# Selective scan with channels and states on partitions, inputs spread by DMA

## The chip, the cores and the metric

One core of a Trainium2 chip. The metric is the device time of one execution in microseconds (us), as the median of several. Kernels are compared only within the same rounds. On one core, a run is called slow when it lies over 1.5% above the fastest of its kernel.

## The reference

Eight images of 256 channels and 32 x 32 pixels go through four layers, each behind a group norm and with a residual: attention of 8 heads, two 3x3 convolutions, and a mixer. The mixer has, per image, four Mamba branches of 64 channels (128 inside), then gates, pointwise products and another attention. The part that matters here, once per branch and image (32 times):

```python
dA  = jnp.exp(dt[..., None] * A)                 # 128 channels x 16 states
dBu = (dt * u)[..., None] * Bm[:, :, None, :]
def step(h, inp):                                # over 1024 pixels
    dA_t, dBu_t, C_t = inp
    h = dA_t * h + dBu_t
    return (h, jnp.einsum('bds,bs->bd', h, C_t))
```

## The kernel before

One state at a time, 128 channels on the partitions, all in float32. Per state: B comes by DMA as one row copied to 128 partitions; ScalarE makes the decays; TensorE makes C on all partitions in PSUM; GpSimd forms dt*u*B; VectorE scans and multiplies by C; TensorE adds the states up through an identity.

```python
def spread(s):
    hs, da, c_all = work("hs"), work("da"), big_tile()
    nc.sync.dma_start(out=hs[:, 0:N], in_=b_rows[s : s + 1].to_broadcast([P, N]))
    nc.scalar.activation(da[:, 0:N], dd, AF.Exp, scale=a_neg[:, ...])      # cut
    for h in range(2):
        nc.tensor.matmul(c_all[:, HALVES[h]], mxpw[...].to_broadcast([P, P]),
                         u[:, HALVES[h]], start=True, stop=True)           # cut
    nc.gpsimd.tensor_mul(hs[:, 0:N], du[:, 0:N], hs[:, 0:N])
    return hs, da, c_all
# for each of 16 states:
nc.vector.tensor_tensor_scan(hh, da[:, 0:N], hh, 0.0, ALU.mult, ALU.add)
nc.vector.tensor_mul(hh, hh, c_all)
for h in range(2):
    nc.tensor.matmul(y_acc[:, HALVES[h]], ident, hs[:, HALVES[h]],
                     start=s == 0, stop=s == DS - 1)
```

SBUF work tiles come from one pool of 20.

Of the kernel before, what the change touches and what calls it, by code (L numbers as in the profile page):

```python
# [17 lines left out]
P = 128  # L18
C = 256
# [9 lines left out]
def preact_stack(ctx: ExitStack, tc: tile.TileContext, I, out, cols):  # L29
    """Per image: attention, two 3x3 convs and the Mamba/attention mixer, each behind a  # L30
    GroupNorm and with a residual. Channels lie on partitions (two tiles of 128)."""
    nc = tc.nc
# [29 lines left out]

# [1 line left out]
    x_next = load_x(0)  # L64
# [36 lines left out]
    make_identity(nc, ident)  # L101
    # 1/8 on the blocks of a normalization group's eight channels
    gmat = wp.tile([P, P], F32, name="gmat")
# [27 lines left out]
    nc.vector.tensor_scalar_mul(a_neg, a_neg, -1.0)  # L131
# [1 line left out]
    def rsqrt_of(t, eps):  # L133
        """1/sqrt(t + eps) in place."""
        nc.vector.tensor_scalar_add(t, t, eps)
        nc.scalar.activation(t, t, AF.Sqrt)
        nc.vector.reciprocal(t, t)

    def channel_stats(srcs):
        """Mean and variance over the pixels, [P, tile, 2]."""  # L140
        mv = sp.tile([P, 2, 2], F32, tag="mv", name="mv")
        for t, src in enumerate(srcs):
            st = sp.tile([P, 2, 6], F32, tag="st", name="st")
            for h in range(2):
                nc.vector.bn_stats(st[:, h], src[:, HALVES[h]])
            nc.vector.bn_aggr(mv[:, t], st.rearrange("p a b -> p (a b)"))
        return mv
# [27 lines left out]
    def layer_norm(srcs, dsts, finish):  # L175
        """Over the channels of each token; finish(t, half, normed) ends a part in place."""
        sq = []
# [58 lines left out]
    def depthwise3(dst, src, wname, bname, i):  # L236
        """Three taps along the tokens; src has a zero before and behind them."""
        nc.vector.tensor_scalar(
            dst, inner(src), col(wname, 3 * i + 1), col(bname, i), ALU.mult, ALU.add
        )  # L240
        for k in (0, 2):
            nc.vector.scalar_tensor_tensor(
                dst, src[:, k : k + N], col(wname, 3 * i + k), dst, ALU.mult, ALU.add
            )

    def project(w, srcs, evac):
        """evac(m, half, psum) for both output tiles of w.T @ srcs."""
        last = len(srcs) - 1
        for m in range(2):
            for h in range(2):  # L250
                ps = mm_tile()
                for k, src in enumerate(srcs):
                    nc.tensor.matmul(  # L253
                        ps,
                        w[:, k, m * P : (m + 1) * P],
                        src[:, HALVES[h]],
                        start=k == 0,
                        stop=k == last,
                    )
                evac(m, HALVES[h], ps)  # L260

    def attention(heads):
        """softmax(q' k) v, a tile of 128 queries at a time: scores with queries on
        partitions, transposed probabilities for the product with v. The scores run one tile
        ahead of the transposes, and these one ahead of the products. Each head gives q, k,
        v by key tile, the rows of its output, and what takes half of that from PSUM."""

# [51 lines left out]

# [1 line left out]
    def layer0(xt):  # L321
# [17 lines left out]
        def rows_of(first, name):  # L339
            """128 rows of q or k, and the inverse of their norms over the tokens."""  # L340
            a = work(name)
# [63 lines left out]

# [1 line left out]
    def padded(name):  # L407
        """A zero-bordered image."""
        t = work(name)
        im = t.rearrange("p (h w) -> p h w", w=34)  # L410
        nc.gpsimd.memset(im[:, 0], 0.0)  # L411
        nc.gpsimd.memset(im[:, 33], 0.0)
        nc.gpsimd.memset(im[:, 1:33, 0:1], 0.0)
        nc.gpsimd.memset(im[:, 1:33, 33:34], 0.0)
        return im
# [41 lines left out]

# [1 line left out]
    def mamba(i, xn, xm):  # L459
        """One branch: 64 channels of xn, through a selective scan, into those of xm."""  # L460
        j, rows = i // 2, slice((i % 2) * 64, (i % 2) * 64 + 64)
# [36 lines left out]

        # B and the low-rank part of dt; B goes through memory to every partition
        low = work("low")  # L500
        for h in range(2):
# [4 lines left out]
            nc.scalar.copy(low[0:36, HALVES[h]], ps[0:36])  # L506
        b_rows = dp.tile([DS, N], F32, tag="b_rows", name="b_rows")
        nc.sync.dma_start(out=b_rows, in_=low[0:DS, 0:N])

        # dt = softplus(a) = max(a, 0) + log1p(e), e = exp(-|a|);  # L510
        # log1p(e) = ln(w) + (e - (w - 1)) with w = fl(1 + e)
        a, e, dt = work("a"), work("e"), work("dt")
# [15 lines left out]
        nc.gpsimd.tensor_mul(du[:, 0:N], dd, uu)  # L528

        y_acc = acc_tile()  # L530

        def spread(s):
            """B and C of a state on every partition, and the state's decays."""
            hs, da, c_all = work("hs"), work("da"), big_tile()
            nc.sync.dma_start(
                out=hs[:, 0:N], in_=b_rows[s : s + 1].to_broadcast([P, N])
            )
            nc.scalar.activation(  # L538
                da[:, 0:N], dd, AF.Exp, scale=a_neg[:, i * DS + s : i * DS + s + 1]
            )  # L540
            at = DS + s
            for h in range(2):
                nc.tensor.matmul(  # L543
                    c_all[:, HALVES[h]],
                    mxpw[:, 0, i, at : at + 1].to_broadcast([P, P]),
                    u[:, HALVES[h]],
                    start=True,
                    stop=True,
                )
            nc.gpsimd.tensor_mul(hs[:, 0:N], du[:, 0:N], hs[:, 0:N])  # L550
            return hs, da, c_all

        ahead = spread(0)
        for s in range(DS):
            hs, da, c_all = ahead
            hh = hs[:, 0:N]
            if s + 1 < DS:
                ahead = spread(s + 1)
            nc.vector.tensor_tensor_scan(hh, da[:, 0:N], hh, 0.0, ALU.mult, ALU.add)  # L559
            nc.vector.tensor_mul(hh, hh, c_all)  # L560
            for h in range(2):
                nc.tensor.matmul(  # L562
                    y_acc[:, HALVES[h]],
                    ident,
                    hs[:, HALVES[h]],
                    start=s == 0,
                    stop=s == DS - 1,
                )
        nc.vector.scalar_tensor_tensor(
# [19 lines left out]
    def mixer_attention(x2):  # L589
        """Eight heads of 32 channels over x2; gives their concatenation."""  # L590
        v = vp.tile([P, NKT, C], F32, tag="v", name="v3")
# [31 lines left out]
        def head(i):  # L623
            t, rows = i // 4, slice((i % 4) * 32, (i % 4) * 32 + 32)

            def take(half, acc):
                # The weights of a query sum to one, so v's bias is the output's.
                nc.vector.tensor_scalar_add(
                    o[t][rows, half], acc, col("ain_b", 4 + t, rows)
                )  # L630
# [12 lines left out]
    def layer3(xt, b):  # L643
# [12 lines left out]

        # gate of each branch
        q4 = work("q4")
# [31 lines left out]

        # residual branch of the gated channels
        rd = [work("rd0"), work("rd1")]
# [18 lines left out]

        # fusion with the normed input
        fd = []
# [18 lines left out]

        # local and global paths
        o = mixer_attention(x2)
# [18 lines left out]

        # per-channel norm, depthwise 3x3, projection
        mv = channel_stats(xo)
# [54 lines left out]
def _arrays(a):  # L810
    """The inputs laid out as the program reads them, and the columns of `vec` by name."""
    c = np.ascontiguousarray

    def tiles(v):
        """[k * 128, n] -> [128, k * n]: channel tiles side by side."""
        v = v.reshape(v.shape[0], -1)
# [6 lines left out]
    def per_state(v):  # L823
        """[4, 128, n] -> [128, 4 * n]."""
        v = v.reshape(NB, P, -1)
        return v.transpose(1, 0, 2).reshape(P, -1)
# [9 lines left out]
        "dtb": per_state(w3("m_dtb")),  # L836
        "alog": per_state(w3("m_alog")),
        "mD": per_state(w3("m_d")),
# [15 lines left out]
    def conv_w(w):  # L854
# [10 lines left out]
        "wc2": conv_w(a["L2_conv_kernel"]),  # L865
        # [branch in pair, channel] x pair x output
        "minw": c(
# [35 lines left out]
```

## Time and profile before

| what | before |
|---|---|
| median | 12,490 us (5 runs, 12,478 to 12,502) |
| loop of 16 states, mean of 32 branches | 96.6 us (94.7 to 100.3) |
| serial part between two loops | 35.9 us |
| mean granted clock of TensorE | 0.893 |

"Loop" is here and below the time from the end of GpSimd's product dt*u, which closes a branch's preparation, to the start of its product with z, which follows the sum over the states. Both are rows of GpSimd's timeline. The lines that carry this are in the prediction. Columns are the window, its length, busy time of PE, PEld, DVE, ACT and POOL with instruction counts, the granted clock, the busy share of the 16 DMA engines, and GB/s.

### The profile page before, as it was taken

Reading aid. Unit: us, or ns where it says so; the run is one execution under the profiler, and the core shown is the slowest. Engines: PE = TensorE matmul, PEld = TensorE weight load, DVE = VectorE, ACT = ScalarE, POOL = GpSimd, SP = SyncE. Lnnn points to the kernel's source line nnn. Section 1 sums busy time; section 2 is a strip of 40 time slices with the busy share of each in tenths; the row PEclk is TensorE's granted clock in tenths of the full one; section 3 lists DMA queues with packets and bytes.
Section 4 is the critical chain, followed back from the end, with each engine's and each line's share of the span. In section 5 each row is a group of like instructions: output and inputs, shape, how many; then the busy total and the mean of one; then the engine's idle time right before and its main releaser. Section 6 shows DMA issues by size and latency. Waiting matters only on the chain.

```text
span 12492.4 us, 97411 instructions
## 1 busy us (share of the span) xinstructions
PE 10370.0 (83%) x39872; PEld 5392.3 (43%) x39872; DVE 6906.5 (55%) x7582; ACT 3176.7 (25%) x4691; POOL 2180.4 (17%) x1012
## 2 busy tenths in 40 slices
PE   9867898678986789867898688986789868898688
PEld 5423554235542355423553235532355323553235
DVE  5365553655536555365553655536555365553655
ACT  3122331223312233122331223312233122331223
POOL 0142001420014200142001420014200142001420
PEclk9888999789988899888998889987899888998889
DMA  1010000100001000010000100001000010000100
GB/s 39 17 64 27 1 7 18 64 28 1 7 20 62 28 2 7 21 60 27 2 6 22 59 28 2 6 22 59 28 2 7 22 59 27 2 2 22 59 27 4
DMA packets 86327, 303.59 MB, mean 24 GB/s; under 512 B 9844, under 2 KB 12532, under 8 KB 85368
## 3 DMA queue, kind: packets, MB, share of 16 engines
q1 hardware_dynamic: 85880, 297.36, 6.9%
q8 instruction: 314, 5.14, 0.2%
q14 instruction: 133, 1.09, 0.0%
HBM read 286.83 MB, written 10.49 MB: 24 GB/s over the span
## 4 chain that ended last, share of the span: by engine, by line
PE 71%; DVE 16%; issue 7%; POOL 3%; ACT 3%; DMA 0%; DVEq 0%; POOLq 0%; ACTq 0%
PE big L272 17%; PE mm L304 16%; PE acc L292 9%; PE mm L430 8%; DVE hs L559 7%; PE acc L562 4%; PE mm L253 3%; PE big L543 3%; PE mm L346 2%; DVE hs L560 2%; POOL hs L550 1%; DVE u L494 1%; DVE dw L782 1%; PE mm L503 1%; PE mm L330 1%
## 5 line engine op out<-in xcount | busy, mean ns | idle before, releaser
L562 PE MATMUL acc<-hs,ident 128*128 128x512 f32 x2048 | 1212.6, 726 | 1257.8 <-DVE hs L560 1257.8
L272 PE MATMUL big<-k,q 64*128 64x512 f32 (+1 forms) x4096 | 2215.9, 640 | 24.1 <-ACT p L283 24.1
L304 PE MATMUL mm<-pt,v 128*64 128x128 f32 (+1 forms) x16384 | 2137.4, 277 | 0.0
L304 PEld LDWEIGHTS mm<-pt,v 128*64 128x64 f32 (+1 forms) x16384 | 1703.4, 124 | 721.1 <-issue 537.5
L559 DVE TENSOR_TENSOR_SCAN hs<-da,hs 128x1024 f32<-128x1024 f32 x512 | 1830.0, 3605 | 214.5 <-POOL hs L550 207.8
L550 POOL TENSOR_TENSOR hs<-a,hs 128x1024 f32<-128x1024 f32 x512 | 1885.7, 3711 | 243.4 <-DMA hs<-b_rows 217.7
L280 DVE TENSOR_REDUCE top<-big 128x1 f32<-128x1024 f32 x1024 | 1253.7, 1224 | 1143.7 <-PE big L272 1134.4
L283 ACT ACTIVATE p<-big,top 128x1024 f32<-128x1024 f32 x1024 | 1140.7, 1114 | 2501.2 <-DVE top L280 2053.5
L562 PEld LDWEIGHTS acc<-hs,ident 128*128 128x128 f32 x2048 | 437.5, 224 | 1896.9 <-DVE hs L560 1450.5
L292 PEld LDWEIGHTS acc<-ident,p 128*128 128x128 f32 x8192 | 901.7, 143 | 713.1 <-issue 704.5
L292 PE MATMUL acc<-ident,p 128*128 128x128 f32 x8192 | 1144.1, 284 | 0.0
L294 DVE COPY pt<-acc 128x512 f32<-128x512 f32 x1024 | 703.7, 687 | 774.1 <-PE acc L292 773.1
L543 PE MATMUL big<-u,w_mxpw 128*128 128x512 f32 x2048 | 1079.1, 656 | 0.0
L430 PE MATMUL mm<-im,w_wc 128*128 128x512 f32 x2304 | 1023.6, 607 | 29.2 <-DVE im L166 25.6
L538 ACT ACTIVATE da<-dt,a_neg 128x1024 f32<-128x1024 f32 x512 | 563.6, 1142 | 1647.2 <-DVE hs L559 1460.2
L272 PEld LDWEIGHTS big<-k,q 64*128 64x128 f32 (+1 forms) x4096 | 650.6, 187 | 583.4 <-issue 546.0
L560 DVE TENSOR_TENSOR hs<-hs,big 128x1024 f32<-128x1024 f32 x512 | 616.8, 1207 | 428.7 <-PE big L543 421.9
L295 ACT COPY pt<-acc 128x512 f32<-128x512 f32 x1024 | 595.4, 581 | 916.2 <-DVE pt L294 893.3
L285 DVE TENSOR_SCALAR p<-p,total 128x1024 f32<-128x1024 f32 x1024 | 769.7, 752 | 28.8
L543 PEld LDWEIGHTS big<-u,w_mxpw 128*128 128x128 f32 x2048 | 454.0, 223 | 654.1 <-issue 654.1
L430 PEld LDWEIGHTS mm<-im,w_wc 128*128 128x128 f32 x2304 | 445.7, 194 | 595.2 <-issue 595.2
L411 POOL MEMSET im<- 128x34 f32 x32 | 7.0, 218 | 3421.3 <-ACT pt L295 3386.8
(183 smaller groups left out, 6068.0 us busy)
## 6 DMA issues: line engine op xcount, KB each, us to landing
hs<-b_rows SPq DMA_DIRECT2D x512, 512.0 KB, 4.1
xt<-in_x SPq DMA_DIRECT2D x8, 1024.0 KB, 4.8
out<-xt SPq DMA_DIRECT2D x32, 256.0 KB, 2.0
w_wc<-in_wc SPq DMA_DIRECT2D x4, 1152.0 KB, 12.2
b_rows<-low SPq DMA_DIRECT2D x32, 64.0 KB, 1.9
w_wqkv<-in_wqkv SPq DMA_DIRECT2D x2, 768.0 KB, 6.9
w_ainw<-in_ainw SPq DMA_DIRECT2D x2, 384.0 KB, 3.9
w_wout<-in_wout SPq DMA_DIRECT2D x4, 128.0 KB, 7.2
```

Of the source, the lines that this page charges most:

```text
L272: nc.tensor.matmul(s[:, HALVES[h]], head["q"][:, qt * P : (qt + 1) * P], head["k"][:, HALVES[h]], start=True, stop=True,)
L280: nc.vector.reduce_max(top, s, axis=AX.X, negate=True)
L283: nc.scalar.activation(p, s, AF.Exp, bias=top, accum_out=total)
L285: nc.vector.tensor_scalar_mul(p, p, total)
L292: nc.tensor.transpose(ps[:, cols_kt], u["p"][:, cols_kt], ident)
L304: nc.tensor.matmul(acc[:, (qt % 4) * P : (qt % 4 + 1) * P], head["v"](kt), u["pt"][:, kt * P : (kt + 1) * P], start=kt == 0, stop=kt == NK ...
L430: nc.tensor.matmul(image(ps), w[:, c, 3 * dy + dx, m * P : (m + 1) * P], im[c][:, 16 * h + dy : 16 * h + dy + 16, dx : dx + 32], start=n == 0,
L543: nc.tensor.matmul(c_all[:, HALVES[h]], mxpw[:, 0, i, at : at + 1].to_broadcast([P, P]), u[:, HALVES[h]], start=True, stop=True,)
L550: nc.gpsimd.tensor_mul(hs[:, 0:N], du[:, 0:N], hs[:, 0:N])
L559: nc.vector.tensor_tensor_scan(hh, da[:, 0:N], hh, 0.0, ALU.mult, ALU.add)
L560: nc.vector.tensor_mul(hh, hh, c_all)
L562: nc.tensor.matmul(y_acc[:, HALVES[h]], ident, hs[:, HALVES[h]], start=s == 0, stop=s == DS - 1,)
```

## The change

Its intent: put 8 channels x 16 states on the partitions. Then B and C need to be spread only once per branch, C no longer comes from TensorE, the decays can go to PSUM (which frees the scan from one SBUF operand), and the sum over states is a product with a 128x32 selection. In exchange dt and dt*u must be spread 16-fold over partitions, for each of 16 groups, through memory. The core of the diff (comments removed by the change, the constants `sel`, the layout of `alog` and some helper lines cut; `...` stands for lines left out):

```diff
-        b_rows = dp.tile([DS, N], ...)
-        nc.sync.dma_start(out=b_rows, in_=low[0:DS, 0:N])
+        bc_rows = dp.tile([2, DS, N], ...)
+        for k in range(2):
+            nc.sync.dma_start(out=bc_rows[k], in_=low[k * DS : (k + 1) * DS, 0:N])
+            t = work("bc")
+            nc.sync.dma_start(out=t[:, 0:N],
+                              in_=bc_rows[k].unsqueeze(0).to_broadcast([8, DS, N]))
...
+        d_rows = dp.tile([2, P, N], F32, tag="d_rows", name="d_rows")
+        nc.sync.dma_start(out=d_rows[0], in_=dd)
+        nc.sync.dma_start(out=d_rows[1], in_=du[:, 0:N])
+        def spread(g):
+            dtr, hs = work("dtr"), work("hs")
+            for k, t in enumerate((dtr, hs)):
+                rows = d_rows[k, g * 8 : g * 8 + 8]
+                nc.sync.dma_start(out=t[:, 0:N],
+                                  in_=rows.unsqueeze(1).to_broadcast([8, DS, N]))
+        def inputs(g, dtr, hs):
+            da = big_tile()                                   # PSUM
+            nc.scalar.activation(da, dtr, AF.Exp, scale=a_neg[:, at : at + 1])
+            nc.gpsimd.tensor_mul(hs, hs, bc[0])
+        order = [g + 4 * c for g in range(4) for c in range(4)]
...     # spread runs three groups ahead
+            nc.vector.tensor_tensor_scan(hs, da, hs, 0.0, ALU.mult, ALU.add)
+            nc.vector.tensor_mul(hs, hs, bc[1])
...     # for each pair of groups
+                        nc.tensor.matmul(y_acc[32 * c : 32 * c + 32, HALVES[h]],
+                                         sel[:, r], t[:, HALVES[h]],
+                                         start=r == 0, stop=r == 3)
```

More of the change, by code (lines that the diff above doesn't have):

```diff
@@ L131, in preact_stack @@
     nc.vector.tensor_scalar_mul(a_neg, a_neg, -1.0)
+    sel = wp.tile([P, 4, 32], F32, name="sel")
+    nc.gpsimd.memset(sel, 0.0)
+    for r in range(4):
+        block = sel[:, r, 8 * r : 8 * r + 8]
+        nc.gpsimd.memset(block, 1.0)
+        for base, sign in ((0, 1), (15, -1)):
+            nc.gpsimd.affine_select(
+                out=block,
+                in_=block,
+                compare_op=ALU.is_ge,
+                fill=0.0,
+                base=base,
+                pattern=[[-16 * sign, 8]],
+                channel_multiplier=sign,
+            )
     def rsqrt_of(t, eps):
@@ L506, in mamba @@
             nc.scalar.copy(low[0:36, HALVES[h]], ps[0:36])
-        b_rows = dp.tile([DS, N], F32, tag="b_rows", name="b_rows")
-        nc.sync.dma_start(out=b_rows, in_=low[0:DS, 0:N])
+        bc_rows = dp.tile([2, DS, N], F32, tag="bc_rows", name="bc_rows")
+        bc = []
+        for k in range(2):
+            nc.sync.dma_start(out=bc_rows[k], in_=low[k * DS : (k + 1) * DS, 0:N])
+            t = work("bc")
+            nc.sync.dma_start(
+                out=t[:, 0:N], in_=bc_rows[k].unsqueeze(0).to_broadcast([8, DS, N])
+            )
+            bc.append(t[:, 0:N])
         a, e, dt = work("a"), work("e"), work("dt")
@@ L528, in mamba @@
         nc.gpsimd.tensor_mul(du[:, 0:N], dd, uu)
+        d_rows = dp.tile([2, P, N], F32, tag="d_rows", name="d_rows")
+        nc.sync.dma_start(out=d_rows[0], in_=dd)
+        nc.sync.dma_start(out=d_rows[1], in_=du[:, 0:N])
         y_acc = acc_tile()
-        def spread(s):
-            hs, da, c_all = work("hs"), work("da"), big_tile()
-            nc.sync.dma_start(
-                out=hs[:, 0:N], in_=b_rows[s : s + 1].to_broadcast([P, N])
-            )
-            nc.scalar.activation(
-                da[:, 0:N], dd, AF.Exp, scale=a_neg[:, i * DS + s : i * DS + s + 1]
-            )
-            at = DS + s
-            for h in range(2):
-                nc.tensor.matmul(
-                    c_all[:, HALVES[h]],
-                    mxpw[:, 0, i, at : at + 1].to_broadcast([P, P]),
-                    u[:, HALVES[h]],
-                    start=True,
-                    stop=True,
-                )
-            nc.gpsimd.tensor_mul(hs[:, 0:N], du[:, 0:N], hs[:, 0:N])
-            return hs, da, c_all
@@ L553, in mamba @@
-        ahead = spread(0)
-        for s in range(DS):
-            hs, da, c_all = ahead
-            hh = hs[:, 0:N]
-            if s + 1 < DS:
-                ahead = spread(s + 1)
-            nc.vector.tensor_tensor_scan(hh, da[:, 0:N], hh, 0.0, ALU.mult, ALU.add)
-            nc.vector.tensor_mul(hh, hh, c_all)
-            for h in range(2):
-                nc.tensor.matmul(
-                    y_acc[:, HALVES[h]],
-                    ident,
-                    hs[:, HALVES[h]],
-                    start=s == 0,
-                    stop=s == DS - 1,
-                )
+        def spread(g):
+            dtr, hs = work("dtr"), work("hs")
+            for k, t in enumerate((dtr, hs)):
+                rows = d_rows[k, g * 8 : g * 8 + 8]
+                nc.sync.dma_start(
+                    out=t[:, 0:N],
+                    in_=rows.unsqueeze(1).to_broadcast([8, DS, N]),
+                )
+            return dtr[:, 0:N], hs[:, 0:N]
@@ new lines, in inputs @@
+        def inputs(g, dtr, hs):
+            da = big_tile()
+            at = i * DS + g
+            nc.scalar.activation(da, dtr, AF.Exp, scale=a_neg[:, at : at + 1])
+            nc.gpsimd.tensor_mul(hs, hs, bc[0])
+            return da
+        order = [g + 4 * c for g in range(4) for c in range(4)]
+        ahead = [spread(g) for g in order[:3]]
+        da_next = inputs(order[0], *ahead[0])
+        ready = []
+        for n, g in enumerate(order):
+            hs = ahead.pop(0)[1]
+            da = da_next
+            if n + 3 < DS:
+                ahead.append(spread(order[n + 3]))
+            if n + 1 < DS:
+                da_next = inputs(order[n + 1], *ahead[0])
+            nc.vector.tensor_tensor_scan(hs, da, hs, 0.0, ALU.mult, ALU.add)
+            nc.vector.tensor_mul(hs, hs, bc[1])
+            ready.append((g, hs))
+            if len(ready) == 2:
+                for h in range(2):
+                    for g2, t in ready:
+                        c, r = g2 // 4, g2 % 4
+                        nc.tensor.matmul(
+                            y_acc[32 * c : 32 * c + 32, HALVES[h]],
+                            sel[:, r],
+                            t[:, HALVES[h]],
+                            start=r == 0,
+                            stop=r == 3,
+                        )
+                ready = []
@@ L836, in _arrays @@
         "dtb": per_state(w3("m_dtb")),
-        "alog": per_state(w3("m_alog")),
+        "alog": w3("m_alog").reshape(NB, 16, P).transpose(2, 0, 1).reshape(P, -1),
         "mD": per_state(w3("m_d")),
```

## The prediction

In it, k is the number of DMA engines that serve one transfer. That an outermost dimension of 8 gives eight engines was my estimate; no transfer of the kernel before tests it.

> **What bounds the kernel now.** I read the whole-span page first (PE 83% busy, 24 GB/s of DMA), then the costliest groups for the lines that the change touches, then the timeline of GpSimd and VectorE in the first image, then the chain of waits and the stage table through one Mamba branch. An eighth of the span is one image; its Mamba part (four branches) runs from 560 us to about 1090 us. The change is confined to it, so the page's 83% for PE, mostly attention, says nothing about it. The groups of the scan loop:
>
> ```profile
> L562 PE MATMUL acc<-hs,ident 128*128 128x512 f32 x2048 | 1212.6, 726 | 1257.8 <-DVE hs L560 1257.8
> L559 DVE TENSOR_TENSOR_SCAN hs<-da,hs 128x1024 f32<-128x1024 f32 x512 | 1830.0, 3605 | 214.5 <-POOL hs L550 207.8
> L550 POOL TENSOR_TENSOR hs<-a,hs 128x1024 f32<-128x1024 f32 x512 | 1885.7, 3711 | 243.4 <-DMA hs<-b_rows 217.7
> L543 PE MATMUL big<-u,w_mxpw 128*128 128x512 f32 x2048 | 1079.1, 656 | 0.0
> L538 ACT ACTIVATE da<-dt,a_neg 128x1024 f32<-128x1024 f32 x512 | 563.6, 1142 | 1647.2 <-DVE hs L559 1460.2
> L560 DVE TENSOR_TENSOR hs<-hs,big 128x1024 f32<-128x1024 f32 x512 | 616.8, 1207 | 428.7 <-PE big L543 421.9
> ```
>
> See that scan and GpSimd multiply average 3.6 and 3.7 us, though alone they take 2.3 each (next fence). The branch's rhythm, GpSimd's timeline (start, duration; L528 makes dt*u just before the loop, L574 multiplies by z just after it):
>
> ```profile
> 682.60 2.34 POOL L574 TENSOR_TENSOR u<-u,z 128x1024 f32<-128x1024 f32 x1 [26.12 <-DVE u L569]
> 717.42 2.35 POOL L528 TENSOR_TENSOR a<-dt,u 128x1024 f32<-128x1024 f32 x1 [1.34 <-DVE dt L526]
> 814.59 2.34 POOL L574 TENSOR_TENSOR u<-u,z 128x1024 f32<-128x1024 f32 x1 [25.82 <-DVE u L569]
> 847.41 2.35 POOL L528 TENSOR_TENSOR a<-dt,u 128x1024 f32<-128x1024 f32 x1 [1.34 <-DVE dt L526]
> 946.42 2.34 POOL L574 TENSOR_TENSOR u<-u,z 128x1024 f32<-128x1024 f32 x1 [29.25 <-DVE u L569]
> ```
>
> From the end of L528 (719.77) to L574 (814.59) is 94.8 us of loop; from L574 to the next end of L528 (849.76) is 35.2 us of serial work. The four loops of this image take 95.0, 94.8, 96.7 and 99.2 us, mean 96.5. So 32 branches x 132 us are a third of the time. Inside a loop, three VectorE rows and the chain:
>
> ```profile
> 612.73 11.86 DVE L559 TENSOR_TENSOR_SCAN hs<-da,hs 128x1024 f32<-128x1024 f32 x3
> 656.51 2.29 DVE L559 TENSOR_TENSOR_SCAN hs<-da,hs 128x1024 f32<-128x1024 f32 x1 [1.10 <-POOL hs L550]
> 667.44 1.22 DVE L560 TENSOR_TENSOR hs<-hs,big 128x1024 f32<-128x1024 f32 x1 [2.21 <-PE big L543]
> ```
>
> ```profile
> 660.53 1.72 PE acc L562 x4
> 662.25 1.72 PE big L543 x4
> 663.97 1.72 PE acc L562 x4
> 665.68 1.72 PE big L543 x4
> ```
>
> Up to about 650 us VectorE is full with slow scans (11.86 us for three) while GpSimd runs; after the last scan the multiplies by C are left over and go at PE's pace, one per 3.44 us (eight products of 0.43). The loop is so first a VectorE/GpSimd loop, then a PE loop. DMA, by windows of 1 us (last two columns: share of 16 engines, GB/s), in the burst that opens a loop:
>
> ```profile
> 578.00:579.00 1.00, 0.29 (x1) 0.00 (x0) 1.00 (x1) 0.00 (x0) 0.00 (x0) 1.00 1.03 397
> 579.00:580.00 1.00, 0.00 (x0) 0.00 (x0) 0.04 (x1) 0.88 (x1) 0.00 (x0) 1.00 1.01 414
> 580.00:581.00 1.00, 0.00 (x0) 0.00 (x0) 0.00 (x0) 0.99 (x2) 0.00 (x0) 1.00 1.04 426
> ...
> hs<-b_rows SPq DMA_DIRECT2D x512, 512.0 KB, 4.1
> xt<-in_x SPq DMA_DIRECT2D x8, 1024.0 KB, 4.8
> b_rows<-low SPq DMA_DIRECT2D x32, 64.0 KB, 1.9
> ```
>
> Sixteen busy engines move 414 GB/s (second row), 25.9 each, so a 4 KB row costs an engine 0.158 us. A 512 KB broadcast is 128 rows, eight per engine: 1.27 us, plus the 1.9 us that the 64 KB write shows as fixed, is 3.2, the shortest landing of its kind in the trace (3.2, median 4.1, longest 8.7).
>
> [...] All large transfers of before have 128 or 16 outermost, and agree with k = 16; none tests a smaller k. [...] scans (two SBUF inputs) take 2.26 to 4.48 us, the multiply with one PSUM input 1.19 to 1.22 always. [...]
>
> **The change part by part.**
> Removed: the C products L543, 16 x 4 x 0.43 = 27.5 us of PE per branch, and with them the PE-paced tail (about 20 us, 661 to 681). PE keeps four products per group, 1.72 us[...]: no longer a bound.
> Moved: exp writes PSUM, so the scan has one SBUF input and should stay at 2.3 us. The multiply by C now reads two SBUF tiles, and it is the one that contends. If GpSimd's 2.35 and this 1.2 exclude each other, the loop's engine floor is 3.55 us per group (VectorE alone 2.3 + 1.2 = 3.5), against the 94.8/16 = 5.9 of before.
> Added: per group two broadcasts of 512 KB in place of one per state. Their source is [8 channels, 16 copies, 1024], outermost 8; the target has 128 partitions. [...] Then 128 rows over eight engines are 16 x 0.158 = 2.53 us each, and a group needs 5.06 us of DMA. That is above the 3.55 us of the engines: DMA becomes the bound. 16 groups: 81 us per branch.
> Added on the path: dt and dt*u go to memory first. dt is ready at 717.35; 512 KB over 16 engines land 3.2 us later, 720.6 (estimate); the first spread is issued then and moves bytes about 1.1 us later (the first broadcast of before was issued at 573.5 and DMA is busy from about 574.5), 721.7. dt*u lands at about 723, behind the first dt spread, so it costs no more than the 1.3 us its own write takes from the rings.
> B and C broadcasts (4 to 5 us each) are issued from 571.5 on and have until 587: hidden.
> Sum for one branch, on the clock of the second branch of the first image: stream 721.7 + 81 (+1.3) = 803 to 804; its completion 0.8; then the last group's GpSimd 2.35, scan 2.3, multiply 1.2: 810 to 811; eight products of the last pair wait for both groups, 3.5 us at full clock, 7 at half (PE is now mostly idle): 814 to 818; the final add 1.28: 815 to 819. Counted from 719.77 that is 96 to 99 us, where before had 94.8, mean 96.5. The serial 35 us are the same code and I expect no hoisting: the next branch's first product waited for the previous output product before, and still does. So per branch -1 to +3 us, times 32: -30 to +100 us. The 20 us of tail and the contention are won, and given back to DMA.
>
> **The rivals.**
> A: k is 16 after all[...]. DMA is 2.53 us per group, the loop is bound by VectorE[...] at 3.55 to 4.2: first scan at 728.5, 57 to 67 us of loop, about 7 of tail and add, 793 to 803, so 13 to 23 us per branch: 420 to 740 us, about 11,900. For it: nothing in the trace contradicts 16, the prefetch of three groups and the pairing for column groups look like work of somebody who saw gains.[...]
> B: DMA-bound and worse: the SP queue is in order, and it waits for free tiles. Nine tiles are held (six of the layer, u, B, C), some eight by four groups, of 20. If the stream runs dry for 1 us per group, 16 us per branch, 500 us: about 13,000. Against: dt's tile is free right after exp, so two groups can stay in flight.
> C: half the engines run faster per engine when the others are idle. Against: rows cost about the same 0.15 us at low load; even 5% gives only 4 us per branch, 130 us in all, 12,370.
> D: PE's clock drops after the loops. A few microseconds per image; ignored.
>
> **Range and chances.** DMA on eight engines I give 0.75: 12,460 to 12,600, with B and C around it. Rival A 0.2. Weighting them, 12,510 us as the point, low 11,880 for A, high 12,700 for a mild B. Faster by over 2% (below 12,245): 0.27, nearly all A and a little C; slower by over 2% (above 12,745): 0.13, B; within 2%: 0.60.
>
> **What would show it.** Landing of a spread of 512 KB alone about 4.5 us and not 3.2; DMA share in the loop stuck near 0.5 at about 205 GB/s; GpSimd and VectorE waiting for hs and dt transfers; loop 96 to 99 us between the dt*u product and the z product. Scans all near 2.3 us and multiplies by C between 1.2 and 3.5[...]. If the loop shows 400 GB/s bursts and scans back to back, A holds and the engine count was the wrong step. If DMA share is well under 0.5 with both engines idle, B. If L574 to the next dt*u is not 35 us, my claim of no hoisting fails.

## More of the kernel before

One more view belongs here: the first microseconds of the burst that opens a loop.

```profile
575.00:576.00 1.00, 1.00 (x4) 0.31 (x2) 0.00 (x0) 0.99 (x1) 0.00 (x0) 1.00 0.85 250
576.00:577.00 1.00, 1.00 (x3) 0.45 (x3) 0.00 (x0) 1.00 (x1) 0.00 (x0) 1.00 0.94 340
577.00:578.00 1.00, 1.00 (x4) 0.22 (x2) 0.88 (x2) 0.06 (x1) 0.00 (x0) 1.00 1.02 365
```

Divide the last column by 16 times the one before it: 18.4, 22.6 and 22.4 GB/s per busy engine. The prediction shows only what comes after, where it is 24 to 26. The engines begin slowly and get faster, with the same kind of transfer.

## The result, and the profile after

| what | before | after |
|---|---|---|
| median of 5 runs | 12,490 us | 13,589 us (13,439 to 13,649) |
| loop, mean of 32 (min to max) | 96.6 us (94.7 to 100.3) | 125.8 us (100.0 to 148.6) |
| serial part | 35.9 us | 36.5 us |
| bytes moved by the main queue | 297 MB | 635 MB |

The ratio is 1.0853, with a 95% interval of 1.0802 to 1.0904. Ratios here are the mean time of one kernel's fast runs over that of the other's of the same rounds, so not quite the ratio of the medians. The loops account for it: 32 x (125.8 - 96.6) = 934 us of the 944 us between the two profiled spans (13,436.8 and 12,492.4). The profiled run is the fastest of the changed kernel's five, and one of the five (13,649 us) counts as slow, so the loops of a median run are longer still.

The groups of the loop, on the page of the changed kernel (line, engine, operation | busy us, mean ns | idle before, releaser):

```profile
L590 DVE TENSOR_TENSOR_SCAN hs<-big,hs 128x1024 f32<-128x1024 f32 x512 | 1170.4, 2286 | 1868.7 <-POOL hs L576 1820.8
L576 POOL TENSOR_TENSOR hs<-hs,bc 128x1024 f32<-128x1024 f32 x512 | 1218.8, 2380 | 2506.2 <-DMA hs<-d_rows 2082.8
L575 ACT ACTIVATE big<-dtr,a_neg 128x1024 f32<-128x1024 f32 x512 | 572.3, 1118 | 3017.4 <-DMA dtr<-d_rows 3009.4
L591 DVE TENSOR_TENSOR hs<-hs,bc 128x1024 f32<-128x1024 f32 x512 | 896.0, 1750 | 17.5
```

Scans are at 2.29 us and GpSimd at 2.38, where both had 3.6 to 3.7: the scan, now with one SBUF input, no longer slows beside GpSimd (2.28 to 2.29 us for all 512, where it took 2.26 to 4.48 with two). Now ScalarE idles 3,009 us for dt's transfers and GpSimd 2,083 us for those of dt*u, and VectorE waits for GpSimd. DMA is the bound. But how uneven it is, GpSimd's timeline of two branches shows (L553 closes the preparation, L610 follows the loop):

```profile
582.94 2.34 POOL L553 TENSOR_TENSOR a<-dt,u 128x1024 f32<-128x1024 f32 x1 [1.34 <-DVE dt L551]
...
621.66 2.34 POOL L576 TENSOR_TENSOR hs<-hs,bc 128x1024 f32<-128x1024 f32 x1 [5.80 <-issue]
629.82 2.34 POOL L576 TENSOR_TENSOR hs<-hs,bc 128x1024 f32<-128x1024 f32 x1 [5.82 <-issue]
...
676.70 2.34 POOL L576 TENSOR_TENSOR hs<-hs,bc 128x1024 f32<-128x1024 f32 x1 [2.70 <-DMA hs<-d_rows]
681.68 2.34 POOL L576 TENSOR_TENSOR hs<-hs,bc 128x1024 f32<-128x1024 f32 x1 [2.64 <-DMA hs<-d_rows]
...
703.75 2.34 POOL L610 TENSOR_TENSOR u<-u,z 128x1024 f32<-128x1024 f32 x1 [9.68 <-DVE u L605]
738.01 2.34 POOL L553 TENSOR_TENSOR a<-dt,u 128x1024 f32<-128x1024 f32 x1 [1.40 <-DVE dt L551]
888.12 2.34 POOL L610 TENSOR_TENSOR u<-u,z 128x1024 f32<-128x1024 f32 x1 [8.72 <-DVE u L605]
```

The same loop takes a group every 8.16 us at first and every 4.98 us later; the first branch's loop lasts 118 us, the second's 148. The windows of the same stretches (columns as above):

```profile
602.00:604.00 2.00, 0.85 (x1) 0.18 (x2) 1.10 (x1) 0.25 (x1) 0.00 (x0) 0.50 0.51 127
604.00:606.00 2.00, 1.07 (x2) 0.00 (x0) 0.00 (x0) 0.00 (x0) 0.69 (x1) 0.50 0.53 131
...
660.00:662.00 2.00, 2.00 (x5) 0.36 (x2) 1.97 (x2) 0.00 (x0) 0.75 (x1) 0.50 0.51 207
662.00:664.00 2.00, 1.34 (x2) 0.00 (x0) 2.00 (x1) 0.32 (x1) 1.60 (x1) 0.50 0.52 211
```

The busy share is one half in both (0.51 to 0.53): eight engines of sixteen, all the time. Yet they move 127 to 131 GB/s in the one state and 207 to 211 in the other. Per engine that is 15.5 and 25 GB/s, or 0.26 and 0.16 us for a row of 4 KB. The second is what the prediction counted with; the first it didn't foresee. Below, these are the slow and the fast state of the rows (not to be mixed up with a slow run). Some loops change from the one to the other, others, like the second here, stay slow to the end.

TensorE's mean granted clock fell to 0.796; in the loop's windows above it is 0.50. It isn't the cause: in attention (300 to 400 us) the granted clock is 1.00 before and after.

### The profile page after: what moved, and what is told of

Same layout as the page of the kernel before. It is cut to its first block, busy times and chain, and to the rows that moved or that the text cites. A ratio compares the mean times of both kernels' runs of the same rounds, so it can differ in the third digit from the quotient of the medians.

```text
span 13436.8 us, 95063 instructions
## 1 busy us (share of the span) xinstructions
PE 9641.9 (72%) x37824; PEld 4698.0 (35%) x37824; DVE 6549.7 (49%) x7582; ACT 3273.1 (24%) x4755; POOL 1513.8 (11%) x1025
## 5 line engine op out<-in xcount | busy, mean ns | idle before, releaser
L597 PE MATMUL acc<-hs,sel 128*32 128x512 f32 x2048 | 1390.2, 1047 | 2931.4 <-DVE hs L591 2931.4
L590 DVE TENSOR_TENSOR_SCAN hs<-big,hs 128x1024 f32<-128x1024 f32 x512 | 1170.4, 2286 | 1868.7 <-POOL hs L576 1820.8
L597 PEld LDWEIGHTS acc<-hs,sel 128*32 128x32 f32 x2048 | 184.2, 149 | 4131.9 <-DVE hs L591 3068.0
L576 POOL TENSOR_TENSOR hs<-hs,bc 128x1024 f32<-128x1024 f32 x512 | 1218.8, 2380 | 2506.2 <-DMA hs<-d_rows 2082.8
L575 ACT ACTIVATE big<-dtr,a_neg 128x1024 f32<-128x1024 f32 x512 | 572.3, 1118 | 3017.4 <-DMA dtr<-d_rows 3009.4
L591 DVE TENSOR_TENSOR hs<-hs,bc 128x1024 f32<-128x1024 f32 x512 | 896.0, 1750 | 17.5
L162 DVE BATCH_NORM_STATS2 st<-xt 128x6 f32<-128x512 f32 x128 | 87.5, 686 | 515.2 <-POOL xt L463 507.2
```

The costliest lines, as they stand in the source:

```text
L576: nc.gpsimd.tensor_mul(hs, hs, bc[0])
L590: nc.vector.tensor_tensor_scan(hs, da, hs, 0.0, ALU.mult, ALU.add)
L591: nc.vector.tensor_mul(hs, hs, bc[1])
L597: nc.tensor.matmul(y_acc[32 * c : 32 * c + 32, HALVES[h]], sel[:, r], t[:, HALVES[h]], start=r == 0, stop=r == 3,)
```

## The experiments

Two questions: is it the eight engines that bind, and what makes a row cost 0.26 us? Every kernel below passed the comparison with the reference. So did the three with a result wrong (e2, e3, e8), so that comparison is too loose here to vouch for the scan; the layouts of the others I checked by working out which channel and state each partition gets.

### Sixteen engines

e1 makes the state the outer index of a partition (p = 8*state + channel), so that the source's outermost dimension is 16.

```diff
-                    in_=rows.unsqueeze(1).to_broadcast([8, DS, N]),
+                    in_=rows.unsqueeze(0).to_broadcast([DS, 8, N]),
```

(B, C, `sel` and `alog` are permuted to match.)

> States outermost on the partitions (partition = 8*state + channel), so every broadcast has an outer dimension of 16 and not 8; bytes, rows and correct result unchanged. Theory 'eight engines[...]': DMA share in the loop goes above 0.5, a group needs 2.5 to 4.2 us of DMA, loop 60 to 80 us in place of 102 to 150, kernel 11,650 to 12,050 us. Rival 'the source sets the pace, 8 rows in memory that everybody reads': rate stays at 128 to 210 GB/s, kernel near 13,400.

Measured: 12,178 us, ratio 0.9757, which is 10% under the changed kernel and faster than before. Loops 83.5 to 88.4 us. A window of its loop:

```profile
620.00:630.00 10.00, 5.63 (x9) 0.72 (x8) 9.93 (x5) 2.24 (x2) 5.67 (x3) 0.60 1.03 243
```

Share 1.03, where the changed kernel has 0.51 to 0.53: sixteen engines. But 243 / (16 x 1.03) = 14.7 GB/s each: the slow state, in all its loops (of all rows, 1% take under 0.17 us). The loop was expected at 60 to 80 us and came at 86, since only the number of engines was mended.

e3 halves the bytes instead: dt is spread once per branch (wrong result).

```diff
+        dtr0 = work("dtr")
-            dtr, hs = work("dtr"), work("hs")
+            dtr, hs = dtr0, work("hs")
+                if k == 0 and g:
+                    continue
```

> The changed kernel with dt spread once per branch and not for each of its 16 groups: half the DMA bytes, all else the same (result wrong on purpose). If DMA is the bound of the loop, a group needs 2.5 to 4.1 us of DMA and the loop falls from 126 to between 62 and 80 us, kernel 11,450 to 12,000; then VectorE with GpSimd at 3.6 to 4.7 us is the floor. If something else holds the loop it stays over 13,000.

Measured: 12,105 us, loops 83.8 to 88.5, mean 85.2. DMA bound it is; that the loop didn't go under 80 again comes from the row: in the windows of its first loop the share is 0.52 at 128 to 134 GB/s, so 4.1 us for one broadcast, or 0.26 us per row: the slow state again, and GpSimd's products do come every 4.1 us there. VectorE is full beside it (9.95 of 10 us from 610 to 620), so how short the loop would be with fast rows isn't shown.

### Is it the source? Rows in memory

e2 keeps eight engines and the SBUF side, and reads 128 different rows (wrong result).

```diff
-        d_rows = dp.tile([2, P, N], F32, ...)
+        d_rows = dp.tile([2, 8, DS + 1, N], F32, ...)      # written [:, 0:DS]
-                    in_=rows.unsqueeze(1).to_broadcast([8, DS, N]),
+                    in_=d_rows[k, :, 0:DS],
```

> Still eight engines, same SBUF side, but the source is 128 different rows (result wrong on purpose). Rival 'one engine reading one 4 KB row of memory sixteen times is slow': each row now takes 0.16 us everywhere, loops near 102 us, kernel 12,600 to 12,800. [...] nothing changes, loops 102 to 150 us in a mix, kernel 13,400 to 13,650.

Measured: 12,824 us (1.0276). Between the two: 25 of 32 loops last at most 106.3 us, but single ones reach 145 and 148. So the slow state doesn't need repeated rows, but the source changes how long it lasts. The edit also puts the rows of different engines 68 KB apart (17 rows of 4 KB), as e9 does later without new rows, so which of the two helped isn't separated.

e6 sets the rows 4,608 bytes apart, e7 does so with sixteen engines.

```diff
-        d_rows = dp.tile([2, P, N], F32, tag="d_rows", name="d_rows")
+        d_rows = dp.tile([2, P, N + 128], F32, tag="d_rows", name="d_rows")
```

> The changed kernel with one edit: the rows of dt and dt*u lie 4,608 bytes apart in memory, not 4,096 (each broadcast row still 4 KB; eight engines; SBUF side untouched; result correct). Theory 'memory side[...]': slow stretches vanish, 0.16 us per row, loops near 98 to 102 us, kernel 12,530 to 12,700. [...] unchanged mix, 13,400 to 13,650.

> The sixteen-engine version with the same padding. There the sixteen engines ran at 0.27 us per row, 244 GB/s, the whole time. Theory 'memory side': rows return to 0.16 to 0.20 us, over 330 GB/s, a group needs 2.5 to 3.2 us of DMA, loop 70 to 78 us, kernel 11,650 to 11,900. [...] stays at 12,180.

Measured: 13,312 us (1.0662; loops 99 to 151, mean 124.1) and 12,177 us (0.9752). The mix stays in e6, though its ratio is 0.019 under the changed kernel's and its median a little under the 13,400 expected; e7 is unchanged. Rows that begin at the same place of a 4 KB step are not the main reason.

e8 has sixteen engines and reads one row 128 times, as the kernel before did (wrong).

```diff
-                rows = d_rows[k, g * 8 : g * 8 + 8]
+                row = d_rows[k, g * 8 : g * 8 + 1]
-                    in_=rows.unsqueeze(0).to_broadcast([DS, 8, N]),
+                    in_=row.to_broadcast([P, N]),
```

> The sixteen-engine version, but every broadcast reads one row 128 times, as the kernel before did, in place of eight rows 16 times each (result wrong on purpose, SBUF side untouched). In before such transfers reached 414 GB/s. If the source's rows matter: over 330 GB/s here too, kernel under 11,950. If the SBUF side or the load alone sets the 244 GB/s: stays at 12,180.

Measured: 11,922 us (0.9552), loops 72 to 87, mean 78.0. The window that answers to e1's:

```profile
610.00:620.00 10.00, 5.86 (x10) 0.85 (x10) 9.90 (x7) 2.85 (x3) 9.34 (x4) 0.66 1.00 342
```

342 GB/s, where e1 has 243: the source matters. (Its pattern is also simpler than e1's, and the issue fell from 0.51 to 0.32 us. No run shows whether the engines fill the same partitions as in e1.) It also hints at the floor of the engines, since DMA now runs ahead (share 0.34 in the window 640 to 650): about 78 us, as the prediction's rival A had it (73 to 83 when its end times are counted from 719.77).

e9 and e10 leave the reading pattern as it is and put the eight rows of a group 68 KB apart.

```diff
-        d_rows = dp.tile([2, P, N], F32, tag="d_rows", name="d_rows")
-        nc.sync.dma_start(out=d_rows[0], in_=dd)
+        d_rows = dp.tile([2, 8, 17, N], F32, tag="d_rows", name="d_rows")
+        nc.sync.dma_start(out=d_rows[0, :, 0:DS].rearrange("c g n -> g c n"), in_=dd)
-                rows = d_rows[k, g * 8 : g * 8 + 8]
+                rows = d_rows[k, :, g]
```

> The changed kernel, eight engines, SBUF side untouched, but the eight rows that a group's broadcast reads lie 68 KB apart in memory in place of 4 KB (correct result). Theory 'memory side: neighbouring rows that several engines read at once hold each other up': slow stretches go, loops 98 to 104 us, kernel 12,500 to 12,720. Theory 'SBUF side alone': mix stays, 13,250 to 13,650.

> The sixteen-engine version with the rows 68 KB apart. Theory 'memory side': rows at 0.16 to 0.20 us, over 300 GB/s, loops 74 to 80 us as with one row, kernel 11,850 to 12,000. Otherwise it stays at 12,180.

Measured: e9 12,590 us (1.0083), loops 97.8 to 100.3, all of them; e10 12,201 us (0.9774), loops 83.6 to 89.9, no gain. In e9 the slow state is not gone, it is short:

```profile
590.00:592.00 2.00, 0.00 (x0) 0.00 (x0) 0.00 (x0) 0.00 (x0) 0.00 (x0) 0.50 0.50 154
592.00:594.00 2.00, 0.00 (x0) 0.00 (x0) 0.00 (x0) 0.00 (x0) 0.00 (x0) 0.50 0.52 164
594.00:600.00 6.00, 0.00 (x0) 0.00 (x0) 0.23 (x1) 1.29 (x2) 2.34 (x1) 0.50 0.51 199
600.00:610.00 10.00, 1.92 (x2) 0.18 (x2) 7.70 (x4) 2.08 (x3) 5.41 (x2) 0.50 0.51 208
```

This loop starts slow and leaves that state after some microseconds, as before's burst did. With sixteen engines the same edit does nothing, so "near rows are slow" is not the whole either. The edit also changes the write of dt and dt*u just ahead of the stream (its issue takes 0.56 to 0.60 us, in place of 0.34), as e2's does; whether that write sets the engines apart was not tested.

### Is it the order of partitions?

What the edits so far left alone is the order in which a broadcast fills the partitions of its tile. That the engines get in each other's way on that side was my guess; which partitions an engine fills, and in what order, no run shows. So I cut the broadcasts up, each time with eight engines and the same rows:

```diff
 # e4: four DMAs of 32 neighbouring partitions
+  out=t[32 * q : 32 * q + 32, 0:N], in_=rows.unsqueeze(1).to_broadcast([8, 4, N])
 # e5: four DMAs, partitions 4 apart
+  out=t[q:P:4, 0:N],                in_=rows.unsqueeze(1).to_broadcast([8, 4, N])
 # e12: two DMAs of 64 neighbouring partitions
+  out=t[64 * q : 64 * q + 64, 0:N], in_=rows.unsqueeze(1).to_broadcast([8, 8, N])
 # e13: two DMAs, partitions 2 apart
+  out=t[q:P:2, 0:N],                in_=rows.unsqueeze(1).to_broadcast([8, 8, N])
```

> Each broadcast cut into four DMAs of 32 contiguous partitions, still eight engines[...] (layout and result adapted, result correct). [...] no slow stretches, 0.16 us per row throughout, about 205 GB/s, loops near 100 us, kernel 12,500 to 12,750. Rival 'source' or 'eight engines as such': the mix stays, 13,400 to 13,650. Possible spoiler: eight DMA issues per group cost the SP queue about 4.6 us, close to the 5.06 us of the transfers.

> Control for the one before: also four DMAs of 32 partitions and eight engines per broadcast, but the partitions of one DMA lie 4 apart[...]. [...] slow stretches stay, 13,300 to 13,700. If it is as fast as e4, cutting into four is what helps[...].

Measured: e4 12,780 us (1.0239), loops all 105 to 106; e5 12,534 us (1.0041), loops all 96.8 to 98.8. e4's slow stretches are gone, as expected (94% of its rows take under 0.17 us), and its time is the spoiler: the SP queue issues almost without a gap, 2.68 us of each 2.8 for four. But e5, meant as the slow control, is the faster of the two and sits inside the prediction's 96 to 99 us. A window of e5, to set beside the 127 to 131 GB/s of the changed kernel:

```profile
600.00:610.00 10.00, 5.53 (x8) 0.71 (x8) 5.56 (x3) 2.23 (x2) 4.86 (x2) 0.50 0.51 202
```

My expectation of it missed. Either the order of partitions 4 apart is what helps, or the pacing by the issue (2.40 us of each 2.5) keeps the engines apart. The next runs tell these from each other:

> Each broadcast as two DMAs of 64 contiguous partitions, eight engines, neighbouring rows; 4 issues per group are 2.4 us of the SP queue, so issue does not pace the engines as it did at four DMAs per broadcast. If cutting a broadcast up is what cures the slow stretches: loops near 98 to 102, kernel 12,500 to 12,700. If it was the pacing by the issue, the slow stretches are back: over 12,900.

> As the one before, but the 64 partitions of a DMA lie 2 apart[...]. If the order in which an engine walks the partitions matters (the four-way strided version was fast), this one is faster than the contiguous halves: near 12,530 against over 12,900. If not, the two are alike.

> The four-way strided version, with dt's transfers issued from ScalarE's queue, so that neither queue's issue time (4 x 0.61 us per 5 us) paces the engines. If the pacing by the single queue kept the slow stretches away: they are back, over 12,800. If it is the order of partitions: stays near 12,530.

e11 is e5 with dt's transfers issued by ScalarE's queue (`nc.scalar.dma_start` where k is 0). Measured: e12 13,196 us (1.0510), e13 12,986 us (1.0408), e11 12,543 us (1.0048) with loops of 97.4 to 101.4. So the pacing isn't it: e11 has half the issues per queue and stays fast. Nor does cutting in two cure it: e12 keeps the mix (101 to 146, in a profile of its slow run; its fast runs took 13,048 and 13,196 us). The order of partitions matters: in e13 the slow state itself is less slow (median of the rows over 0.2 us: 0.22 us, 0.26 in e12). By their times e12 and e13 are not clearly apart (95% intervals of the ratios 1.041 to 1.061 and 1.038 to 1.044). One window of each, e12's first:

```profile
600.00:610.00 10.00, 1.91 (x2) 0.18 (x2) 4.64 (x4) 2.17 (x2) 2.34 (x1) 0.50 0.51 125
```

```profile
600.00:610.00 10.00, 4.79 (x8) 0.72 (x8) 3.65 (x3) 1.12 (x1) 4.22 (x2) 0.50 0.52 151
```

125 GB/s with neighbouring partitions, 151 with partitions 2 apart; e5, with partitions 4 apart, has 178 in its windows from 588 to 592 us (at a share of 0.45 to 0.49) and 193 to 199 from 592 on. e13 was expected near 12,530 and only went a part of the way. Four DMAs of neighbouring partitions without the pacing were not run, so for e5 the order and the cutting in four are not fully separated.

### Are they in step?

e14 starts each branch's stream with two small copies from memory to memory, 6 and 2 outermost, meant to delay the eight engines unequally; e15 has two copies with 8 outermost, meant to delay all eight alike; e16 is e1 with copies of 12 and 4, meant to delay the sixteen unequally. Which engines a copy delays was my estimate; no run shows it. The two copies are written as a loop here:

```diff
+        junk = dp.tile([2, 12, 6, N], F32, tag="junk", name="junk")
+        for j, k in enumerate((6, 2)):                        # e15: (8, 8)
+            nc.sync.dma_start(out=junk[j, 0:k, 0:5],          # e16: (12, 4), 4 rows
+                in_=d_rows[0, 0 : 6 * k].rearrange("(a b) n -> a b n", b=6)[:, 0:5])
```

> The changed kernel plus two small memory-to-memory copies just before the first spread of each branch[...]. Theory 'engines in step': the slow stretches are gone or short, loops 98 to 105 us, kernel 12,530 to 12,800. Rival: 0.26 us comes from the load or the rows, not from step: mix stays, 13,300 to 13,700.

> Control: two copies of the same size per engine, but both on all eight engines, so that all are delayed alike. Theory 'engines in step': mix stays, about 1.5 us more per branch than the changed kernel, 13,300 to 13,750. If it is as fast as the unequal delay, some extra transfer ahead of the stream is what helps, not the unequal start.

> The sixteen-engine version with copies[...]. Theory 'in step[...]': rate from 244 to over 320 GB/s, loops 74 to 80 us, kernel 11,800 to 12,000. If the sixteen are held by something else: 12,180 plus the copies' 1 to 2 us per branch, 12,200 to 12,240.

Measured: e14 12,668 us (1.0140), loops 97.8 to 103.2, all 32; e15 12,791 us (1.0165; fast runs 12,626 and 12,756), in its profile (a slow run) 27 of 32 loops under 110 us, the others up to 150; e16 12,092 us (0.9685), mean loop 83.4, outside the 74 to 80 expected. The windows of e14 (twice) and of e16 (in its first and in its second loop), for the comparison with 602 to 606 us of the changed kernel and with e1:

```profile
592.00:594.00 2.00, 0.00 (x0) 0.00 (x0) 0.00 (x0) 0.00 (x0) 0.00 (x0) 0.50 0.51 186
594.00:596.00 2.00, 0.00 (x0) 0.00 (x0) 0.00 (x0) 1.12 (x1) 0.00 (x0) 0.50 0.51 211
```

```profile
620.00:630.00 10.00, 6.81 (x13) 1.18 (x14) 9.93 (x6) 2.92 (x3) 6.99 (x3) 0.67 1.03 305
740.00:750.00 10.00, 5.37 (x10) 0.87 (x12) 9.93 (x6) 2.46 (x3) 4.68 (x2) 0.67 1.03 237
```

With e14's copies, the long slow stretches are gone with eight engines, while the stream's rows, partitions, bytes and engines are untouched. With sixteen the gain is small: 305 GB/s in the first loop (75 us), short of the 320 expected, but 237 in the second (88 us), no more than e1 has. And e15, which should have changed nothing, also helped in most loops. Its copies may set the engines apart by themselves; as a control it is not clean.

The traces settle what e15 left open. They hold every DMA packet (no view prints them; what follows is worked out from the packed traces), and each engine ends its share of a DMA with a packet of 4 bytes (one broadcast of the changed kernel has eight of them, from 603.4 to 604.2 us); so one can read how many rows apart the eight engines finish a broadcast, though not which engine is which. In the changed kernel's first loop they finish 0, 0.4, 0.5, 0.6, 2.2, 2.5, 2.6 and 2.9 rows after the first of them, unchanged in one broadcast after the other, with rows of 0.26 us. Then one engine falls 5.0 rows behind, and three broadcasts later a row takes 0.159 us. Join the eight to four pairs so that the smallest gap within a pair is as large as it can be (which engines belong together, if any do, no view shows), and all 1,024 broadcasts of the changed kernel sort themselves:

| smallest gap within a pair, in rows | broadcasts | mean row, median (10% to 90%) |
|---|---|---|
| under 1 | 234 | 0.263 us (0.250 to 0.268) |
| 1 to 2 | 288 | 0.257 us (0.226 to 0.262) |
| 2 to 2.5 | 107 | 0.261 us (0.204 to 0.266) |
| 2.5 to 3 | 37 | 0.172 us (0.166 to 0.190) |
| 3 and more | 358 | 0.160 us (0.159 to 0.162) |

So eight engines are slow in step and fast out of step, and about three rows are enough. In e15 the loops of 148 and 150 us have gaps of 0.2 to 0.5 rows from their first broadcast on, while in its first three fast loops the engines end the first broadcast spread over 8 to 12 rows: its equal copies did set them apart.

### A version that beats both

Cutting with a new order of partitions was the cheapest cure with eight engines, so e17 and e18 apply it to sixteen, with nothing ahead of the stream:

```diff
 # e1, each broadcast cut in two (e18: in four, dt's on ScalarE's queue)
+                for q in range(2):
+                    nc.sync.dma_start(
+                        out=t[q:P:2, 0:N],
+                        in_=rows[q:8:2].unsqueeze(0).to_broadcast([DS, 4, N]),
+                    )
```

> The sixteen-engine version, each broadcast of the groups as two DMAs whose 64 partitions lie 2 apart[...]. Theory 'in step[...]': rate between the 244 GB/s of the plain version and 414; 290 to 350, loops 75 to 83 us, kernel 11,850 to 12,080 (with eight engines the same cut took the mean loop from 126 to 113 us). If the order of partitions is nothing to sixteen engines: 12,180.

> As the one before with four DMAs, 4 partitions apart[...]; dt's are issued from ScalarE's queue since one queue could not issue eight per group in time. Theory 'in step[...]': slow state gone as with eight engines, over 330 GB/s while the queue is full, VectorE with GpSimd then the bound, loops 72 to 78 us, kernel 11,750 to 11,950.[...]

Measured: e17 11,850 us, ratio 0.9486 (0.9471 to 0.9502), loops 72 to 83, mean 77.0: 5.1% faster than before, 12.8% below the median of the changed kernel. e18 11,996 us (0.9608), mean loop 81.4. e17's groups and a window:

```profile
L567 POOL TENSOR_TENSOR hs<-hs,bc 128x1024 f32<-128x1024 f32 x512 | 1227.6, 2398 | 927.1 <-DMA hs<-d_rows 545.3 <-DMA dtr<-d_rows 196.8 <-issue 106.3
L582 DVE TENSOR_TENSOR hs<-hs,bc 128x1024 f32<-128x1024 f32 x512 | 835.1, 1631 | 17.6
```

```profile
620.00:630.00 10.00, 7.17 (x13) 1.16 (x14) 9.93 (x6) 2.33 (x3) 6.68 (x3) 0.67 1.04 294
```

GpSimd's wait for transfers of dt*u fell from 2,083 us (1,042 in e1) to 545 us, and VectorE is full (9.93 of 10 us). That alone doesn't show that VectorE is now the bound, since e1's window has 9.93 too, with longer multiplies (mean 2.17 us against 1.63 here). The cut also changes which rows one DMA reads, and a cut in two without the new order was not run with sixteen engines: that the order is what helped is likely, not shown. e18 shows shares of 0.79 to 0.85: its engines are no longer always busy, and its loops are longer (mean 81.4 us against 77.0). It differs from e17 in the cut and in the queue of dt's issues; neither was tested by itself.

### All runs

| kernel | engines | edit | median us | ratio to before | mean loop us |
|---|---|---|---|---|---|
| changed | 8 | - | 13,589 | 1.0853 | 125.8 |
| e6 | 8 | rows 4,608 bytes apart | 13,312 | 1.0662 | 124.1 |
| e12 | 8 | two DMAs, neighbouring partitions | 13,196 | 1.0510 | 121.5 (slow run) |
| e13 | 8 | two DMAs, 2 apart | 12,986 | 1.0408 | 113.4 |
| e2 | 8 | 128 different rows | 12,824 | 1.0276 | 107.8 |
| e15 | 8 | copies of 8 and 8 ahead | 12,791 | 1.0165 | 106.2 (slow run) |
| e4 | 8 | four DMAs, neighbouring partitions | 12,780 | 1.0239 | 105.5 |
| e14 | 8 | copies of 6 and 2 ahead | 12,668 | 1.0140 | 99.7 |
| e9 | 8 | rows 68 KB apart | 12,590 | 1.0083 | 98.7 |
| e11 | 8 | as e5, two queues | 12,543 | 1.0048 | 98.8 |
| e5 | 8 | four DMAs, 4 apart | 12,534 | 1.0041 | 98.1 |
| e10 | 16 | rows 68 KB apart | 12,201 | 0.9774 | 86.7 |
| e1 | 16 | - | 12,178 | 0.9757 | 86.0 |
| e7 | 16 | rows 4,608 bytes apart | 12,177 | 0.9752 | 85.9 |
| e3 | 8 | half the bytes | 12,105 | 0.9695 | 85.2 |
| e16 | 16 | copies of 12 and 4 ahead | 12,092 | 0.9685 | 83.4 |
| e18 | 16 | four DMAs, 4 apart, two queues | 11,996 | 0.9608 | 81.4 |
| e8 | 16 | one row | 11,922 | 0.9552 | 78.0 |
| e17 | 16 | two DMAs, 2 apart | 11,850 | 0.9486 | 77.0 |

Medians are of all runs, ratios of fast runs; the changed kernel and e12 have one slow run each, e15 two of four, so its verdict is unclear. The mean loop is that of the profiled run.

## Why the prediction was wrong

Its mechanism was right and one term of its sum was mis-sized.

- **Removed and moved: right.** The PE-paced tail is gone, scans are at 2.28 to 2.29 us, and the contended instruction is the multiply by C, 1.23 us alone and up to 3.40 beside GpSimd (mean 1.75).
- **Eight engines, DMA as the bound: right.** The busy share is 0.51 to 0.53 through the loop, and 1.03 once the outermost dimension is 16 (e1).
- **No hoisting of the serial part: right.** 36.5 us against 35.9. The tail after the last multiply was 3.72 us, of 3.5 to 7 predicted (with six of its eight products; two had run before the last multiply).
- **The failed step: "a 4 KB row costs an engine 0.158 us", hence "16 x 0.158 = 2.53 us each, and a group needs 5.06 us of DMA".** It was read from the end of a burst, when the rate is best. Measured: 0.16 us in the fast state (4.98 us per group) and 0.26 in the slow one (8.16 us per group), with the loop changing between them at no fixed time. At 0.16 throughout, the loop is 97 to 99 us, as e5 has it, and the kernel at 12,534, inside the 12,460 to 12,600 that the prediction gave for eight engines. The mix made the loop 125.8 us. The extra 27 to 28 us, times 32 branches, are most of the 930 us by which even the profiled run, the fastest of five, lies over the predicted 12,510.
- **The sign that I passed over.** The median broadcast of before landed after 4.1 us and not 3.2; I took the shortest. With 1.9 us fixed, that would be (4.1 - 1.9) / 8 = 0.275 us per row. This is an upper bound, since many broadcasts wait behind another one; by the DMA packets of before's loops a row takes 0.194 us in the mean and 0.159 in the median. The window at the head of the burst (18.4 GB/s, so 0.22 us per row) pointed the same way.
- **The rivals.** Rival C asked if rows could be faster with half the engines; that they could be slower was not asked. (By the packets of before, rows take 0.159 us in the median both with up to four in flight and with 13 to 16.) Rival B foresaw a stream that runs dry; SP does wait for tiles (395 us in all for the exp that frees dt's, 143 us for the products with the selection), but the stream never ran dry (mean share 0.51 to 0.52 while it runs, in each of the 32 loops). Rival A's estimate for sixteen engines, 11,900, is met by sixteen engines once their rows are faster (e8 11,922; e17 11,850, still with 0.24 us per row), while e1 with sixteen slow ones is at 12,178. It was not what the change did. Rival D's drop is short: in windows of 20 us from 1220 us on, after the loops of the first image, the granted clock is 0.70, 0.66 and 1.00, where before has 0.83, 0.74 and 1.00 from 1080 on.

What makes a row slow is narrowed down, not settled. Shown with eight engines: rows are slow while the engines walk in step (0.26 us with gaps under 2.5 rows, 0.16 with 3 and more), and e14's copies end the long slow stretches (loops 97.8 to 103.2 us). A new order of partitions (with a cut; e5, 96.8 to 98.8) and rows further apart (with another write ahead of the stream; e9, 97.8 to 100.3) change the state too; padding by 512 bytes leaves the mix (e6, 99 to 151), and the speed of e5 doesn't hang on issue pacing (e11, 97.4 to 101.4). Why engines in step are slow, no run shows; nor why rows 68 KB apart free eight engines and not sixteen (e9 12,590 us, e10 12,201), or why one row does free sixteen (e8, 342 GB/s where e1 has 243). That the source sets how soon the engines drift apart is argued, not shown.

## What to carry to other kernels

Look at the outermost dimension of a DMA's source: here 8 came with half the engines (share 0.51 to 0.53) and 16 with all of them (1.03), and the transposed order of the same broadcast made the kernel 10% faster. For a stream of transfers, size a row by several windows, the slow ones too (here 0.16 to 0.22 us in one burst), not by the best one, and give the slow case its own line among the rivals. Where the share of DMA is full and the GB/s per busy engine are low, try to change the order in which the partitions are filled before giving up bytes (from e1 to e17: 12,178 to 11,850 us). Count the issues too: one took 0.32 us in the kernel before, 0.51 in e1 and 0.57 in the changed kernel with the queue free, and in e4 (0.64 us each, one every 0.70 us, eight per group) they paced the kernel.
